# A planner's dearer transfers, and the first half batch of layer 0 entered on VectorE

## The chip, the cores and the metric

The kernel runs on one core of a Trainium2 chip, as one launch of one program. The metric is the device time of an execution in microseconds, lower being better; the time of a kernel is the median of several executions. A core has TensorE (matmuls, PE in the profile), VectorE (DVE), ScalarE (ACT), GpSimd (POOL) and SyncE (SP), which here does nothing but issue transfers. Each engine takes its instructions in the order in which they were written into the program and waits on semaphores where it needs another engine's result.

## The reference, cut to what matters

Four layers work on x of 2 batches of 1024 tokens of 128 features. Each normalises x, computes a sequence part s and a feed-forward part g, and adds their product:

```python
for layer in (L0, L1, L2, L3):
    xn = layernorm(x)
    x = x + layer.attn(xn) * silu(layer.ffn(xn))
```

Layer 0's sequence part is a selective recurrence, and its feed-forward part a mixture of eight experts of three products each:

```python
gated = clip(layernorm(x) @ sign(W1).T + b1, -1, 1)
x  = x + gated @ sign(W2).T + b2
qx = quantised(x)                        # by groups of tokens
u  = layernorm(qx)
xs, z = split(u @ in_proj.T)
xs = silu(causal_conv4(xs))
dt, B, C = split(xs @ x_proj.T)
dt = softplus(dt @ dt_proj.T + dt_b)     # 256 channels
h[t] = h[t-1] * exp(dt * A) + dt * xs * B   # 16 states a channel
y  = (h . C + D * xs) * silu(z)
out = qx + y @ out_proj.T
```

Layer 1 is an additive attention and eight gated experts, layer 2 a chunked state-space layer with 32 heads and eight small experts, layer 3 a causal attention and a two-product feed-forward. Only layer 0 has code that the change edits.

## The kernel before

**Layer 0.** The 2048 tokens are 16 tiles of 128, four quarters of 512, or two batches of two halves each. A half batch passes five stages, `take_1` to `take_5`. `take_1` takes the mean and variance of each of its four tiles of qx (`statistics`), the inverse root by three Newton steps (`inverse_root`), and writes `u` = qx * rinv + shift for each tile; then TensorE turns `u` (L632) and it is split into a rounded part `uT_h` and a rest `uT_l`. `take_2` does the convolution as 24 matmuls per half (two sets of 128 channels, four taps, three products each, tile `xz_ps`, helper `mm3` at L621 to L623) and the silu. `take_3` projects to dt, B and C and computes `e = exp(-|dt|)`. `take_4` computes the softplus as max(dt, 0) + ln(1 + e) with a correction `w = e - ((1 + e) - 1)` (L1080, L1081), the products `dt` and `dx` (L1084, L1085), and writes them to DRAM as `Dtd` (L1087), from where they are read back spread over partitions as `dd` (L1230). For the very first half and channel set, `dd` is read from SBUF instead (L1228), and no write stands before it. `take_5` does the gate z.

The recurrence is run in 16 steps a half batch (`inputs`, `step`): each has a product `dBx` = dx * B (L1243 on VectorE, one in four at L1241 on POOL), two exponentials `dA` on ACT (L1251), two scans of 128x512 on VectorE (L1252), two products with C on POOL (L1256) and four narrow matmuls that fold the states (L1263). B reaches the right partitions by a matmul `B_ps` (L1237). 128 scans in all make layer 0.

In `inverse_root`, the inverse root of a variance of four tiles runs Newton's steps on POOL (L595 to L598, four instructions a step); for other widths they run on VectorE (L591 to L593, three a step). `u` is written by POOL (L1007), and so are the two instructions of the softplus's correction.

Beside all this, layer 0's experts run on TensorE and ACT: `first` (L1137), `second` (L1142, L1144), `third` (L1152, L1154, L1156) and `weighted_sum` (L1162) for each of eight experts and four quarters, 32 tasks. Their weights are loaded by L1133. When the last task is done, `moe_end` (L1179 onward) makes the gate, which `layer_end` multiplies in.

**Layers 1 to 3.** Layer 1 of batch 0 begins while layer 0 still scans batch 1. Layer 2 works through 32 blocks (2 batches, 16 blocks of 128 channels), each with transfers of decays and rows (`so`, `cd`, `Srow`, `Mrow`) from DRAM scratch.

**What sets the order.** The program is first written in the order of the code. Then `_issue_order` takes all instructions and lists them anew for each engine. `_operations` gives each instruction a cost (`_price`), its dependences with lags, and, for a transfer, a time on the wire (`op.wire`, bytes by a rate that depends on the kind of source). `_forward` plays the engines with these costs: whenever an engine is free it takes, of its ready instructions, the one with the lowest key; a transfer takes its place on one common wire some time after its issue and is done some time after that, both parts of `_DMA`. `_backward` plays the program from its end, and its times are the next keys. Thirty rounds of this are made, then 300 tries with keys disturbed at random in a stretch of 60 us; the order with the shortest played span is kept and is written into the program as fixed order per engine. All transfers are issued by SyncE, one behind another; one that waits for its buffer or source holds those behind it.

So a changed price of transfers can change the order of every engine in every layer, and an instruction that moves to another engine changes the keys of those before it.

Of the kernel before, what the change touches and what calls it, by code (L numbers as in the profile page):

```python
# [15 lines left out]
ALU = mybir.AluOpType  # L16
# [56 lines left out]
_SAME = {"PE": -160.0, "DVE": 50.0, "Activation": 50.0, "Pool": 100.0, "SP": 0.0}  # L73
_TABLE = 1283.0
_SWITCH = 4000.0
_DMA = 1550.0
_SPELL = 3413.0
_LOW, _HIGH = 0.45, 0.8

# [73 lines left out]
def _operations(nc, slots):  # L153

    ops, users, past = [], {}, {}

    def in_psum(a):
        return a.tensor.name in slots and slots[a.tensor.name][3] == "PSUM"

    for ins in nc.cur_bb.bb.instructions:  # L160
        if type(ins).__name__.startswith("BassTile") or ins.opcode == "RegisterMove":
            continue
        op = _Op(len(ops), ins)
        reads, writes = ([a.bass_ap for a in x if getattr(a, "bass_ap", None) is not None] for x in (ins.ins, ins.outs))
        op.cost = _price(op, reads, writes, in_psum)
        op.table = _table_of(ins)
        op.columns, op.first, op.mate = set(), op, None
        if ins.opcode == "Matmult" and not ins.is_transpose and writes[0].ap[0][1] in (8, 32, 64):
            op.strip, op.area = writes[0].offset // (writes[0].ap[0][0] or 1), 1.0
            op.columns, op.strips = {(op.strip, writes[0].offset)}, {op.strip}  # L170
        op.wire = 0.0
        if op.dma:

            n, rows = 4, 1
            for _, c in writes[0].ap:
                n *= c
            again = any(s == 0 and c > 1 for s, c in reads[0].ap)
            for s, c in list(reads[0].ap)[:-1]:
                rows *= c if s else 1
            inside = reads[0].tensor.name in slots and slots[reads[0].tensor.name][3] != "DRAM"  # L180
            op.wire = n / (430.0 if not again else 200.0 if inside else 300.0 if rows > 2 else 170.0)
        for a, writing in [(a, False) for a in reads] + [(a, True) for a in writes]:
            name = a.tensor.name
            if name not in slots:
                continue
            space = slots[name][3]
            ap = [tuple(v) for v in a.ap]
            p0, p1, f0 = 0, 0, a.offset
            if space != "DRAM":
                row = _elements([(0, 0)] + [(0, d) for d in list(a.tensor.shape)[1:]])  # L190
                p0, f0 = divmod(a.offset, row)
                p1 = p0 + ap.pop(0)[1] - 1
            f1 = f0 + sum(abs(s) * (c - 1) for s, c in ap)
            if space == "PSUM":
                p0, p1, f0, f1 = 0, 127, 0, 4095
            log = past.setdefault(name, [])
            for q0, q1, g0, g1, other, wrote in log:
                if (writing or wrote or space == "PSUM") and other is not op and q0 <= p1 and p0 <= q1 and g0 <= f1 and f0 <= g1:
                    if other.engine != op.engine or other.dma:
                        lag = 0.0 if other.dma else _HOP[op.engine]  # L200
                    else:
                        lag = _SAME[op.engine] if wrote and not writing and op.engine != "PE" else -_AHEAD[op.engine]
                    op.after[other] = max(op.after.get(other, -1e3), lag)
            if writing:
                log[:] = [r for r in log if r[4] is op or not (p0 <= r[0] and r[1] <= p1 and f0 <= r[2] and r[3] <= f1)]
            log.append((p0, p1, f0, f1, op, writing))
            if name not in op.tiles:
                op.tiles.append(name)
                users.setdefault(name, []).append(op)
                if users[name][0] is not op:  # L210
                    op.after.setdefault(users[name][0], -1e3)

        mate = ops[-1] if ops else None
        if op.columns and mate is not None and mate.columns and mate.tiles[-1] == op.tiles[-1] and not mate.columns & op.columns:
            op.columns |= mate.columns
            if op.strip in mate.strips:
                op.cost += 10.0
            else:
                op.strips |= mate.strips
                op.cost = 25.0  # L220
            first = mate.first
            first.after.update({o: max(lag, first.after.get(o, -1e3)) for o, lag in op.after.items() if o.at < first.at})
            mate.mate, op.first = op, first
        ops.append(op)
    for op in ops:
        if op.columns and op.mate is None:
            op.cost += 87.0
    return ops, users
# [30 lines left out]
def _forward(ops, users, slots, behind, key):  # L259
# [22 lines left out]
    table, wire, port = None, 0.0, {"DVE": [0.0, 0.0], "Pool": [0.0, 0.0]}  # L282
# [24 lines left out]
    while events:  # L307
        now, kind, _, op = heapq.heappop(events)
# [17 lines left out]
        e = op.engine  # L326
# [6 lines left out]
        if held:  # L333
            op = mate
            ready[e].remove(held[0])
            heapq.heapify(ready[e])
        elif e == "PE" or e not in ("Activation", "DVE"):
            op = heapq.heappop(ready[e])[2]
        else:
            op = _next(ready[e], table, [max(0.0, t - now) for t in port["Pool"]] if e == "DVE" else (0.0, 0.0))  # L340
# [15 lines left out]
        idle[e] = now + (cost if e == "PE" or op.dma else max(cost - _AHEAD[e], 40.0))  # L356
        done = now + cost + (_AHEAD[e] if e == "PE" else 0.0)
        if op.dma:
            wire = max(wire, now + 0.4 * _DMA) + op.wire
            done = wire + 0.6 * _DMA  # L360
        end[op] = done
        for t in op.tiles:
            if t not in begun:
# [95 lines left out]
def recurrent_d4(ctx: ExitStack, tc: tile.TileContext, x, w0, f0, fwd, w1, w13d, w1y, w2, w2in, w3, r0, r2, r3, out):  # L459
    nc = tc.nc  # L460
# [105 lines left out]
    def tiles_of(b):  # L566
        return range(b * TPB, (b + 1) * TPB)

    def statistics(src, ts):

        n = len(ts)
        st = small.tile([P, n, 6], F32, name=f"ln_st{n}")
        mv = small.tile([P, n, 2], F32, name=f"ln_mv{n}")
        for i, t in enumerate(ts):
            nc.vector.bn_stats(st[:, i, :], src[:, t, :])
            nc.vector.bn_aggr(mv[:, i, :], st[:, i, :])
        return mv, inverse_root(mv[:, :, 1], f"ln{n}")

    def inverse_root(v, name):

        n = v.shape[-1]
        small_pool = n == 4
        x = small.tile([P, n], F32, name=f"{name}_x")
        nc.vector.tensor_scalar(x, v, EPS, None, ALU.add)
        y = small.tile([P, n], F32, name=f"{name}_y")
        yi = y.bitcast(I32)
        nc.vector.tensor_scalar(yi, x.bitcast(I32), 1, None, ALU.arith_shift_right)
        nc.vector.tensor_scalar(yi, yi, -1.0, 1597463007.0, ALU.mult, ALU.add)
        t = small.tile([P, n], F32, name=f"{name}_t")
        for _ in range(0 if small_pool else 3):  # L590
            nc.vector.tensor_tensor(t, y, y, ALU.mult)  # L591
            nc.vector.scalar_tensor_tensor(t, t, -0.5, x, ALU.mult, ALU.mult)
            nc.vector.scalar_tensor_tensor(y, t, 1.5, y, ALU.add, ALU.mult)  # L593
        for _ in range(3 if small_pool else 0):
            nc.gpsimd.tensor_tensor(t, y, y, ALU.mult)  # L595
            nc.gpsimd.tensor_tensor(t, t, x, ALU.mult)
            nc.gpsimd.tensor_scalar(t, t, -0.5, 1.5, ALU.mult, ALU.add)
            nc.gpsimd.tensor_tensor(y, t, y, ALU.mult)  # L598
        return y
# [225 lines left out]
    with ExitStack() as l1, ExitStack() as l0:  # L825
# [52 lines left out]
        with pool_of("l0a") as pa, pool_of("l0b", bufs=2) as pb, pool_of("l0_pre", bufs=5, space=PSUM) as pp:  # L878
# [118 lines left out]
            taken, held = {}, {}  # L997
            halo = pj.tile([P, 2, 3], F32R, name="halo")

            def take_1(b, h, pp, tag):  # L1000

                ts = range(b * TPB + 4 * h, b * TPB + 4 * h + 4)
                mv, rinv = statistics(qx, ts)
                shift = shifted(mv, rinv)
                u = pj.tile([P, 4, D], F32, name="u")
                for j, t in enumerate(ts):
                    nc.gpsimd.tensor_scalar(u[:, j, :], qx[:, t, :], rinv[:, j : j + 1], shift[:, j : j + 1], ALU.mult, ALU.add)  # L1007
                up = [pj.tile([P, 515], F32R, name=f"uT_{n}") for n in "hl"]
                for k, x in enumerate(up):
                    if h:  # L1010
                        nc.gpsimd.tensor_copy(x[:, 0:3], halo[:, k])
                    else:
                        nc.gpsimd.memset(x[:, 0:3].bitcast(F32), 0.0)
                split(turned(pp, u, tag), *(x[:, 3:] for x in up))
                if h == 0:
                    for k, x in enumerate(up):
                        nc.gpsimd.tensor_copy(halo[:, k], x[:, 512:515])
                held["up"] = up
# [52 lines left out]
            def take_4(b, h, pp, tag, fast=False):  # L1071
# [3 lines left out]
                for c in range(2):  # L1075
# [1 line left out]
                    ln = pp.tile([P, 512], F32, name="ln_ps", tag=tag)  # L1077
                    nc.scalar.activation(ln, e, AF.Ln, bias=one_col)

                    nc.gpsimd.tensor_scalar(w[:, c, :], e, 1.0, -1.0, ALU.add, ALU.add)  # L1080
                    nc.gpsimd.tensor_tensor(w[:, c, :], e, w[:, c, :], ALU.subtract)  # L1081
                    nc.vector.tensor_tensor(ln, ln, w[:, c, :], ALU.add)
                    nc.vector.scalar_tensor_tensor(ln, dt, 0.0, ln, ALU.max, ALU.add)
                    nc.scalar.copy(dt, ln)  # L1084
# [23 lines left out]
            routing(0, pp)  # L1108
            mark("first")
            quantise(0)  # L1110
            take_1(0, 0, pp, "mm")
            mark("routing_0")
            routing(1, pp)
            mark("first")
# [933 lines left out]
```

## Time and profile before

| what | value |
|---|---|
| median of three executions | 1190.09 us (1188.87 to 1194.23) |
| the profiled execution | 1188.86 us |
| its span | 1187.1 us |
| TensorE busy | 1020.7 us, 86% |
| VectorE busy | 931.5 us, 78% |
| ACT busy | 866.1 us, 73% |
| POOL busy | 739.2 us, 62% |
| mean granted TensorE clock | 0.939 |
| first scan starts | 126.73 us |
| last sum of layer 0's experts | 273.9 us |
| transfers | 109.09 MB, mean 92 GB/s |

The span is the time from the first to the last recorded instruction. A timeline line holds start, length, engine, code line, operation, what is written and read, count, and in brackets the idle time before it with what ended it. An SPq line is the issue of a transfer, not the transfer itself. A TensorE matmul in plain float32 stands as two records, one with float32r data as one. A busy TensorE under a granted clock below 1 is slower than its busy time says.

### The profile page before, as it was taken

To read this page: it belongs to the slowest core of one execution; us is meant where nothing else is said; L and a number is where in the kernel's file an instruction comes from. 1 tells how busy PE (TensorE), PEld (TensorE's weight loads), DVE (VectorE), ACT (ScalarE), POOL (GpSimd) and SP (SyncE) were. 2 spreads that over 40 slices of the span, in tenths; PEclk is the share of its full clock that TensorE was granted. 3 is DMA by queue.
4 is the path that set the end of the run, shared out by engine and by line. 5 is a ranking of instruction groups with operands and counts; after the bars stand their busy time and mean duration, and the time that the engine had idled before them with its cause. 6 is when DMAs were issued, how large, how long until landed. Compare 5 with 4: busy or idle time off the path is not lost.

```text
span 1187.1 us, 18167 instructions
## 1 busy us (share of the span) xinstructions
PE 1020.7 (86%) x6399; PEld 735.6 (62%) x6399; DVE 931.5 (78%) x1537; ACT 866.1 (73%) x1294; POOL 739.2 (62%) x776
## 2 busy tenths in 40 slices
PE   3997967979376889989779789999998999998998
PEld 2664523435033666778658576867676777776787
DVE  6734798997899896675776488888888999888666
ACT  4556785785877894574847689888898988877654
POOL 6564598895987375232151158797995978899311
PEclk9998997999567989999959899999999999999999
DMA  3003445352552113020030333445354444442000
GB/s 109 8 21 101 125 120 182 123 186 99 189 177 83 51 62 100 1 82 23 5 106 32 87 100 96 111 119 149 101 141 95 125 107 112 107 111 73 19 9 28
DMA packets 58846, 109.09 MB, mean 92 GB/s; under 512 B 6274, under 2 KB 31746, under 8 KB 58628
## 3 DMA queue, kind: packets, MB, share of 16 engines
q1 hardware_dynamic: 58756, 107.93, 31.6%
q8 instruction: 51, 0.84, 0.3%
q14 instruction: 39, 0.32, 0.1%
HBM read 91.52 MB, written 14.29 MB: 89 GB/s over the span
## 4 chain that ended last, share of the span: by engine, by line
PE 34%; DVE 10%; ACT 9%; issue 4%; DMA 3%; POOL 2%; SPq 0%; POOLq 0%; DVEq 0%; ACTq 0%
PE wo_ps L1781 4%; PE yd_ps L1757 3%; PE u_ps L1734 3%; PE yo_ps L1762 3%; DVE h L1419 2%; PE e_ps L1698 2%; PE y_ps L799 2%; DVE st L1735 2%; PE ht_ps L1719 1%; DMA so<-So 1%; PE y_ps L1895 1%; PE y_ps L1646 1%; PE av_ps L1925 1%; ACT e_ps L1699 1%; DVE M L1701 1%
## 5 line engine op out<-in xcount | busy, mean ns | idle before, releaser
L1256 POOL TENSOR_TENSOR hs<-hs,bc 128x512 f32<-128x512 f32 x128 | 161.0, 1278 | 48.6 <-DVE hs L1252 28.8
L1419 DVE SCALAR_TENSOR_TENSOR h<-in_ps,w,h 128x1023 f32<-128x1023 f32 (+2 forms) x96 | 121.1, 1271 | 5.7 <-ACT h L1416 5.5
L1251 ACT ACTIVATE dA<-dd,negA 128x512 f32<-128x512 f32 x128 | 87.4, 688 | 31.8 <-DVE hs L1252 25.4
L1735 DVE TENSOR_TENSOR_SCAN st<-cd,u_ps 128x512 f32<-128x512 f32 x64 | 77.8, 1215 | 19.4 <-PE u_ps L1734 8.7
L1701 DVE SCALAR_TENSOR_TENSOR M<-e_ps,GT 128x1024 f32<-128x1024 f32 x64 | 77.0, 1214 | 10.5 <-ACT e_ps L1699 10.3
L1768 POOL TENSOR_TENSOR h<-h,so 128x384 f32<-128x384 f32 (+1 forms) x64 | 73.0, 1144 | 19.1 <-DVE so L1767 18.6
L1769 POOL TENSOR_TENSOR h<-h,sg 128x512 f32<-128x512 f32 x64 | 82.9, 1300 | 0.8
L1252 DVE TENSOR_TENSOR_SCAN hs<-dA,last,dBx 128x512 f32<-128x512 f32 x64 | 79.9, 1271 | 2.9 <-ACT dA L1251 2.0
L799 PEld LDWEIGHTS y_ps<-w2e,hh 128*128 128x128 f32 x512 | 72.4, 199 | 14.7 <-DVE hh L791 3.8
L799 PE MATMUL y_ps<-w2e,hh 128*128 128x128 f32 x512 | 78.1, 288 | 1.9 <-DVE acc L804 0.9
L1723 POOL TENSOR_TENSOR hdd<-htok,dtd 128x512 f32<-128x512 f32 x64 | 67.1, 1051 | 20.3 <-ACT htok L1722 15.4
L1774 POOL TENSOR_TENSOR ssq<-ssq,so 128x512 f32<-128x512 f32 x60 | 76.6, 1286 | 3.0 <-ACT so L1773 2.9
L1757 PE MATMUL yd_ps<-M,htok 128*64 128x128 f32 x1024 | 70.7, 280 | 8.0 <-DVE M L1701 5.6
L1252 DVE TENSOR_TENSOR_SCAN hs<-dA,dBx 128x512 f32<-128x512 f32 x64 | 75.7, 1211 | 2.1 <-ACT dA L1251 1.1
L1734 PEld LDWEIGHTS u_ps<-hdd,Btok 128*128 128x128 f32 x448 | 63.3, 193 | 16.8 <-issue 6.0
L1762 PE MATMUL yo_ps<-Cf,stc 128*128 128x128 f32 x448 | 70.7, 280 | 2.1 <-DVE h L1765 0.9
L1734 PE MATMUL u_ps<-hdd,Btok 128*128 128x128 f32 x448 | 69.8, 281 | 2.8 <-POOL stc L1737 1.3
L1762 PEld LDWEIGHTS yo_ps<-Cf,stc 128*128 128x128 f32 x448 | 62.3, 191 | 13.4 <-issue 4.7
L1757 PEld LDWEIGHTS yd_ps<-M,htok 128*64 128x64 f32 x1024 | 55.1, 137 | 24.4 <-issue 7.0
L1243 DVE TENSOR_TENSOR dBx<-dd,B_ps 128x1024 f32<-128x1024 f32 x48 | 57.9, 1209 | 12.2 <-PE xz_ps L623 4.7
L1699 ACT ACTIVATE e_ps<-e_ps 128x1024 f32<-128x1024 f32 x64 | 64.3, 1011 | 1.9 <-PE e_ps L1698 1.4
L1263 PE MATMUL y_ps<-hs,fold 128*32 128x512 f32 x256 | 52.9, 758 | 14.1 <-DVE ln_t L591 9.2
(535 smaller groups left out, 3190.7 us busy)
## 6 DMA issues: line engine op xcount, KB each, us to landing
bc<-BCd SPq DMA_DIRECT2D x32, 512.0 KB
cd<-Dd SPq DMA_DIRECT2D x32, 512.0 KB
so<-So SPq DMA_DIRECT2D x64, 256.0 KB
dd<-Dtd SPq DMA_DIRECT2D x28, 512.0 KB
w13f<-in_w13d_dram SPq DMA_DIRECT2D x16, 256.0 KB
Dtd<-dt SPq DMA_DIRECT2D x7, 512.0 KB
fw<-in_fwd_dram SPq DMA_DIRECT2D x16, 192.0 KB
dd<-dt SPq DMA_DIRECT2D x4, 512.0 KB
```

Source lines behind the costliest of these rows:

```text
L799: nc.tensor.matmul(y_ps[:, j * P : (j + 1) * P], hh[:, c, j * P : (j + 1) * P], w2e[:, c * P : (c + 1) * P], start=(c == 0), stop=(c == 1))
L1251: nc.scalar.activation(dA, dd[:, r, 0, :], AF.Exp, scale=negA[:, n, r : r + 1])
L1252: nc.vector.tensor_tensor_scan(hs[:, r, :], dA, dBx[:, r, :], last[:, n, r : r + 1] if h else 0.0, ALU.mult, ALU.add)
L1256: nc.gpsimd.tensor_tensor(hs[:, r, :], hs[:, r, :], cs[:, 0, :], ALU.mult)
L1419: nc.vector.scalar_tensor_tensor(dst[:, n:], ps[:, : S - n], w[:, k : k + 1], dst[:, n:], ALU.mult, ALU.add)
L1701: nc.vector.scalar_tensor_tensor(M, ps, 3.0e38, G, ALU.min, ALU.mult)
L1734: nc.tensor.matmul(pv[:, j, :], Btok[:, c, :], hdd[:, c, :], start=True, stop=True)
L1735: nc.vector.tensor_tensor_scan(st.rearrange("p f j -> p (f j)"), cd[:, half].rearrange("p h w -> p (h w)"), ps, 0.0, ALU.mult, ALU.add)
L1757: nc.tensor.matmul(yd[64 * k : 64 * (k + 1), j * P : (j + 1) * P], htok[:, 4 * q + j, 64 * k : 64 * (k + 1)], Ms[q][:, k, j * P : (j + 1) ...
L1762: nc.tensor.matmul(yo[:, j * P : (j + 1) * P], stc[:, c - 1, :], Cf[:, c * P : (c + 1) * P], start=True, stop=True)
L1769: nc.gpsimd.tensor_tensor(y, y, sg[:, cols], ALU.mult)
L1774: nc.gpsimd.tensor_tensor(ssq[:, cols], ssq[:, cols], so[:, cols], ALU.add)
```

## The change

Two things are edited.

In the planner, the fixed price of a transfer goes from 1550 to 2150 ns; of this, 0.6 instead of 0.4 lie before the wire and 0.4 instead of 0.6 behind it. The rates of the wire fall from 430 to 300 bytes per ns for plain transfers, from 200 to 190 for one spread from SBUF, from 300 to 230 for one spread from many DRAM rows; 170 stays.

In the first half batch of batch 0 alone (`take_1(0, 0, ..., True)` and the `take_4` that was already called with True), Newton's steps, the four instructions that write `u`, and the four of the softplus's correction run on VectorE instead of POOL. All other half batches keep theirs on POOL.

```diff
-_DMA = 1550.0
+_DMA = 2150.0
...
-            op.wire = n / (430.0 if not again else 200.0 if inside else 300.0 if rows > 2 else 170.0)
+            op.wire = n / (300.0 if not again else 190.0 if inside else 230.0 if rows > 2 else 170.0)
...
-            wire = max(wire, now + 0.4 * _DMA) + op.wire
-            done = wire + 0.6 * _DMA
+            wire = max(wire, now + 0.6 * _DMA) + op.wire
+            done = wire + 0.4 * _DMA
...
-    def statistics(src, ts):
+    def statistics(src, ts, fast=False):
...
-        return mv, inverse_root(mv[:, :, 1], f"ln{n}")
-
-    def inverse_root(v, name):
+        return mv, inverse_root(mv[:, :, 1], f"ln{n}", n == 4 and not fast)
+
+    def inverse_root(v, name, aside=False):
...
-        small_pool = n == 4
...
-        for _ in range(0 if small_pool else 3):
+        for _ in range(0 if aside else 3):
...
-        for _ in range(3 if small_pool else 0):
+        for _ in range(3 if aside else 0):
...
-            def take_1(b, h, pp, tag):
+            def take_1(b, h, pp, tag, fast=False):
...
-                mv, rinv = statistics(qx, ts)
+                mv, rinv = statistics(qx, ts, fast)
...
-                    nc.gpsimd.tensor_scalar(u[:, j, :], qx[:, t, :], rinv[:, j : j + 1], shift[:, j : j + 1], ALU.mult, ALU.add)
+                    (nc.vector if fast else nc.gpsimd).tensor_scalar(u[:, j, :], qx[:, t, :], rinv[:, j : j + 1], shift[:, j : j + 1], ALU.mult, ALU.add)
...
-                    nc.gpsimd.tensor_scalar(w[:, c, :], e, 1.0, -1.0, ALU.add, ALU.add)
-                    nc.gpsimd.tensor_tensor(w[:, c, :], e, w[:, c, :], ALU.subtract)
+                    eng = nc.vector if fast else nc.gpsimd
+                    eng.tensor_scalar(w[:, c, :], e, 1.0, -1.0, ALU.add, ALU.add)
+                    eng.tensor_tensor(w[:, c, :], e, w[:, c, :], ALU.subtract)
...
-            take_1(0, 0, pp, "mm")
+            take_1(0, 0, pp, "mm", True)
```

## The prediction

> **What bounds the kernel now.** I read the page first (the span of 1187.1 us, the engines' shares, the chain that ended last), then the busy time of each engine by stage, then the timelines of POOL, VectorE, SyncE's queue and TensorE around the first scan, because the edits stand there. The profiled execution took 1188.86 us, 1.76 us more than its span and 1.23 us less than the median of 1190.09 us.
>
> The busy time by stage (length, then busy us and count of each engine, TensorE's granted clock, DMA share, GB/s):
>
> ```profile
> core 0: us, PE busy (x) PEld busy (x) DVE busy (x) ACT busy (x) POOL busy (x), PEclk, DMA share, GB/s
> ...
> 20.00:82.00 62.00, 57.95 (x348) 39.40 (x348) 38.12 (x101) 36.43 (x67) 42.01 (x81) 1.00 0.05 14
> 82.00:127.00 45.00, 35.33 (x157) 23.22 (x157) 16.25 (x30) 24.39 (x40) 12.60 (x25) 0.89 0.42 109
> 127.00:276.00 149.00, 124.45 (x682) 62.62 (x681) 134.49 (x136) 111.51 (x193) 131.53 (x113) 0.94 0.43 142
> 276.00:400.00 124.00, 83.02 (x335) 41.45 (x334) 111.31 (x163) 95.84 (x160) 91.57 (x70) 0.72 0.39 130
> 400.00:680.00 280.00, 241.90 (x1436) 194.62 (x1435) 192.84 (x459) 183.28 (x279) 92.47 (x103) 0.92 0.19 55
> 680.00:1040.00 360.00, 342.95 (x2498) 263.08 (x2497) 319.20 (x363) 314.46 (x407) 284.79 (x277) 1.00 0.44 113
> ```
>
> The reader is to see three kinds of stage. From 680 to 1040 us (layer 2) TensorE is 95% busy at full clock and bounds. From 127 to 400 us (layer 0's scans) VectorE is 90% busy and TensorE waits at a lower clock. From 20 to 127 us the recurrence has not begun: TensorE is full until 82 us with the expert work of layer 0, then nothing is full; VectorE is 36% busy between 82 and 127. The chain of waits reaches back only to 433 us and says nothing on the start.
>
> What holds the first scan up, on POOL, then VectorE, then SyncE's queue, then TensorE:
>
> ```profile
> 55.06 0.63 POOL L595 TENSOR_TENSOR ln_t<-ln_y 128x4 f32<-128x4 f32 x1
> ...
> 70.61 0.20 POOL L598 TENSOR_TENSOR ln_y<-ln_t,ln_y 128x4 f32<-128x4 f32 x1
> ...
> 72.65 1.75 POOL L1007 TENSOR_SCALAR u<-qx,ln_y,shift 128x128 f32<-128x128 f32 x4
> ...
> 99.75 3.84 POOL L1080 TENSOR_SCALAR sp_w<-sp_e 128x512 f32<-128x512 f32 x2
> 103.55 2.49 POOL L1081 TENSOR_TENSOR sp_w<-sp_e,sp_w 128x512 f32<-128x512 f32 x2
> ```
>
> ```profile
> 50.84 1.89 DVE L1103 TENSOR_SCALAR qx<-qx,rg 128x256 f32<-128x256 f32 x1
> ...
> 104.85 0.70 DVE L1082 TENSOR_TENSOR ln_ps<-ln_ps,sp_w 128x512 f32<-128x512 f32 x1 [4.26 <-POOL sp_w L1081]
> ...
> 109.31 1.28 DVE L1085 TENSOR_TENSOR dt<-ln_ps,xs 128x512 f32<-128x512 f32 x2
> ...
> 125.47 1.22 DVE L1243 TENSOR_TENSOR dBx<-dd,B_ps 128x1024 f32<-128x1024 f32 x1 [4.70 <-PE xz_ps L623]
> 126.73 2.34 DVE L1252 TENSOR_TENSOR_SCAN hs<-dA,dBx 128x512 f32<-128x512 f32 x2
> ```
>
> ```profile
> 110.02 0.33 SPq L1087 DMA_DIRECT2D Dtd<-dt  x1
> 110.62 1.25 SPq L1228 DMA_DIRECT2D dd<-dt  x2
> 112.68 3.30 SPq L1230 DMA_DIRECT2D dd<-Dtd  x1
> 116.02 3.18 SPq L1228 DMA_DIRECT2D dd<-dt  x2
> ```
>
> ```profile
> 70.51 1.12 PE L1142 MATMUL p<-h,fw 128*128 128x512 f32 x2
> ...
> 82.14 0.50 PE L621 MATMUL xz_ps<-uT_h,taps_l 128*128 128x512 f32 x1
> ```
>
> Newton's steps lie on POOL from 55.06 to 70.81 us, twelve instructions of 0.2 us scattered among large ones; `u` follows, and the convolution starts at 82.14. The softplus's sum waits 4.26 us for POOL. dBx at 125.47 is charged to TensorE, but its B_ps matmul was done by 115.9. It also needs both halves of `dd`; the halves of one tile are not issued together (the first pair at 110.62 is the first half of two tiles, the second pair at 116.02 their second halves), so I read this wait as the transfer.
>
> **Part 1, Newton's steps and u on VectorE.** Removed from POOL: 12 instructions and four `u` (1.75 us). Added to VectorE: nine of about 0.17 us (row L593 at 18.3 to 20.4 us), 1.5, and four 128x128 tensor-scalars at 0.25 to 0.34 (row L917), 1.1. In the new order they stand among routing's instructions; counting these with their rows on from the copy of probs at 57.05, the last `u` ends near 61.4 us, not 74.36. But TensorE was full, so what counts is what it does ahead of the convolution. In the built order there are 61 fewer matmuls ahead: nine of L621 to L623 at 0.235 (2.1), three of L1142 at 1.05 (3.2; the row's two records are one matmul), four of L1152 at 0.43 (1.7), thirteen of L1154 at 0.23 (3.0), 32 of L1162 at 0.083 (2.6): 12.6 us. 82.14 becomes 69.5, and u's transposes come up near 63, after 61.4. The two accounts agree, so -12.6 us. Queued behind `u` on VectorE is routing's second maximum; it gets 1.1 us later, beside full TensorE work.
>
> **Part 2, the softplus's sums.** POOL's four instructions took 6.3 us, begun after `u` of the other half. On VectorE two tensor-scalars at 0.41 to 0.48 (rows L1105, L896) and two tensor-tensors at 0.69: 2.3 us, from the end of the exponential at 98.20 to 100.5. Then the logarithm is late: a table load of 1.28 us and a first half that ends at 100.8. So 104.85 becomes 100.8, -4.05. The new order also puts two zs products and a uT_l (107.52 to 109.31, 1.8 us) behind the first L1085. Together -5.9 us for the issue of `dd`. Nothing that stands behind the new instructions on VectorE is needed earlier.
>
> **Part 3, the order of transfers.** In SyncE's queue the first two `dd` now stand ahead of the Dtd write, and the first tile's second half stands before the `dd` that has to wait until Dtd has landed (3.30 us at 112.68). An expert's weight load stands ahead of them and waits for TensorE's eighth third-layer product, which comes some 4 us before by its place in the order. Bounds: 0 (the transfers share the same engines) and -5.4 (116.02 less 110.62). I take -2: the number of 512 KB transfers ahead falls by one, not by all. First scan: 126.73 - 12.6 - 5.9 - 2 = 106.2 us, 20.5 earlier.
>
> **What goes back.** TensorE work ahead of the first B_ps falls by 11.1 us (nine, four, three, twelve and eight of the kinds above); it has to lie beside the scans. There TensorE has 149 - 124.45 = 24.6 us free, part of its busy time is at clock 0.94, and VectorE and POOL have 15 and 17 free. Bounds 0 and +11.1; I take +4, as three engines near 90% can't be interleaved without loss.
>
> **The rest of the plan.** The price moves every instruction's key, so all is ordered anew. The expert sum's end stands behind 66 scans instead of 68, the last scan behind 18 products of layer 1's experts in both, and TensorE's work ahead of the first and of the 256th L1757 is the same within 2 us. The activation tables are loaded 155 times, not 163: 8 x 1.283 us of ACT, which bounds nowhere before 400 us. Bounds for all of this: -10.3 (all loads on the path) and, from the queue in layer 2, +22 (below). I take 0.
>
> Sum: -20.5 + 4 + 0 = -16.5. 1188.86 - 16.5 = 1172.4 for a profiled execution, 1173.6 at the median; I say 1174 us, 1.4% faster.
>
> **A rule against it.** The tensor-scalar L1103 at 50.84 took 1.89 us and ended 0.14 us after POOL's taps_l product (50.22 to 52.59); without POOL beside it the 128x512 form took 0.41. The Trainium skill (SBUF — State Buffer, Who interferes with whom) says that such instructions and GpSimd's take a shared port pair in turn, the loser blocked for the whole instruction; the trace agrees. By that rule each of the six moved tensor-scalars could stand behind a POOL instruction of 1.27 us: 7.6 us, and the sum would be -8.9, 1181 at the median. I keep the rows' uncontended times, since POOL has little left to run there.
>
> **Rivals.** *The gain is eaten beside the scans.* All 11.1 us come back, and port waits or `dd` landing no sooner cost 2 to 5 more: -20.5 + 11.1 + 3 = -6.4, so 1184 (1182 to 1188). For it: 90% on VectorE, 88% on POOL. Against: TensorE's 24.6 us. That the change does not move the scan at all (TensorE stays in the way) speaks against the 61 matmuls; 5.9 us of part 2 would remain, also 1184. *Slower: SyncE's queue in layer 2.* A dearer transfer is issued earlier; at the head of an in-order queue it waits for its buffer, and the loads behind it wait too. SyncE's L1692 waited 97.8 us in 25 waits for its buffer already. Layer 2 has 32 block steps with TensorE 95% busy: each us lost per block costs up to 32. It cancels the gain at 0.5 us a block and is slower by 0.5% from 0.7 (22 us): 1196 to 1205. Against it: TensorE's order there is unchanged.
>
> **The numbers.** Forecast 0.62; eaten, or scan not moved, 0.17; queue 0.17; 0.04 for more gain than forecast, when the chain's 3% of DMA (36 us) shrinks too. The forecast's own range: 1174 with Part 3's -3.4 and no loss (-4) below, 1166, and the whole +11.1 above (+7.1) and +2 of Part 3, 1183. The range reaches down to 1160 and up through the eaten case to the edge of the queue's, 1197. Half a per cent (6 us) is about what this measurement can tell, as the three runs spread by 0.45%. Faster: 0.62 + 0.04 + 0.03 of the eaten case, 0.69; same 0.14; slower 0.17.
>
> **What would show it.** Right: convolution near 70 us, no wait for POOL at L1082, first scan at 104 to 109, expert end near 256 to 262, TensorE's share of the span up by about a point. Wrong: a first scan after 115, a scan stage longer than 153 us, or TensorE under 94% from the first L1757 to the last.

## The result, and the profile after

The changed kernel takes 1203.51 us at the median of four executions (1199.79 to 1208.90), the kernel before 1190.78 us (1188.87 to 1194.23). The ratio is 1.0125, with a 95% interval of 1.0082 to 1.0168: slower by 1.25%. I had forecast 1174 us and a range that ended at 1197. The profiled execution took 1199.79 us, the least of the four; its span is 1198.1 us.

The busy time by stage of the changed kernel (length, then busy us and count of each engine, TensorE's granted clock, DMA share, GB/s). The limits are the first convolution, the first scan, the experts' last sum, 400 us as in the table before, and the first and last L1757:

```profile
core 0: us, PE busy (x) PEld busy (x) DVE busy (x) ACT busy (x) POOL busy (x), PEclk, DMA share, GB/s
20.00:68.00 48.00, 44.62 (x239) 32.57 (x239) 33.08 (x90) 29.88 (x55) 30.11 (x42) 1.00 0.03 9
68.00:109.00 41.00, 34.93 (x195) 23.31 (x195) 20.92 (x56) 23.84 (x39) 13.82 (x43) 0.92 0.46 112
109.00:252.00 143.00, 128.01 (x725) 67.14 (x725) 127.39 (x127) 116.17 (x201) 126.31 (x111) 0.96 0.45 150
252.00:400.00 148.00, 93.34 (x337) 43.97 (x335) 131.53 (x172) 93.93 (x158) 103.03 (x79) 0.69 0.34 116
400.00:683.00 283.00, 239.86 (x1446) 194.95 (x1445) 191.44 (x458) 170.82 (x273) 86.07 (x98) 0.93 0.17 52
683.00:1104.00 421.00, 399.04 (x2887) 303.56 (x2886) 372.49 (x417) 362.01 (x468) 334.81 (x327) 0.99 0.41 109
```

The first two stages are shorter, as forecast (48 and 41 us instead of 62 and 45); the third is shorter too (143 instead of 149), where I had forecast it longer by 4. The fourth starts 24 us earlier and is where the lead is lost: up to 400 us it has 337 matmul records in 148 us at a clock of 0.69, where the kernel before had 335 in 124 us at 0.72. The last one is longer: from the first L1757 to the last 421.5 us instead of 414.4.

The start of the recurrence did what the change says. TensorE's first convolution product, then VectorE's timeline, then SyncE's queue of the changed kernel (start, length, engine, line, operation, tiles, count, idle time before and what ended it; the lines quoted from 583 to 1078 are one less than before):

```profile
68.06 0.50 PE L620 MATMUL xz_ps<-uT_h,taps_l 128*128 128x512 f32 x1
```

```profile
59.31 2.25 DVE L1006 TENSOR_SCALAR u<-qx,ln_y,shift 128x128 f32<-128x128 f32 x4
...
86.81 0.76 DVE L1080 TENSOR_SCALAR sp_w<-sp_e 128x512 f32<-128x512 f32 x2 [1.08 <-ACT sp_e L1067]
...
89.30 1.31 DVE L1082 TENSOR_TENSOR ln_ps<-ln_ps,sp_w 128x512 f32<-128x512 f32 x2 [0.25 <-ACT ln_ps L1077]
...
92.34 0.69 DVE L1085 TENSOR_TENSOR dt<-ln_ps,xs 128x512 f32<-128x512 f32 x1 [0.54 <-ACT dt L1084]
...
107.99 1.22 DVE L1243 TENSOR_TENSOR dBx<-dd,B_ps 128x1024 f32<-128x1024 f32 x1 [3.58 <-DMA dd<-dt]
109.24 2.34 DVE L1252 TENSOR_TENSOR_SCAN hs<-dA,dBx 128x512 f32<-128x512 f32 x2
```

```profile
93.06 1.23 SPq L1228 DMA_DIRECT2D dd<-dt  x2
94.39 4.31 SPq L1087 DMA_DIRECT2D Dtd<-dt  x1
98.75 4.23 SPq L1228 DMA_DIRECT2D dd<-dt  x2
```

The first scan starts at 109.24 instead of 126.73, 17.5 us earlier, and the experts' last sum (L1162) is at 251.5 instead of 273.9. But the first sum of layer 0 into X (L1288), from which layer 1 of batch 0 begins, moves only from 306.85 to 299.96. The gate `g` (L1285) is loaded into the buffer that `bc_rows` of the last half batch holds until it is written out; so it goes by the recurrence's pace, not the experts'.

In SyncE's queue `bc_rows` is written out 12 us earlier (282.75 instead of 294.85) and `g` loaded 10 us earlier (287.64 instead of 297.56). The traces of three runs below with the same order up to there (e9, e11, e12) put this first sum between 298 and 307 us, so the 7 us are themselves uncertain by about as much.

Two sights in the fourth and fifth stage stand out. The first is a VectorE instruction on 128x8 numbers that takes 7 us. VectorE's timeline, then POOL's:

```profile
313.21 6.96 DVE L583 TENSOR_SCALAR ln_x<-ln_mv 128x8 f32<-128x8 f32 x1
320.08 1.21 DVE L1243 TENSOR_TENSOR dBx<-dd,B_ps 128x1024 f32<-128x1024 f32 x1
```

```profile
310.83 6.17 POOL L1256 TENSOR_TENSOR hs<-hs,bc 128x512 f32<-128x512 f32 x5
316.96 0.74 POOL L609 TENSOR_TENSOR qk_w_l<-w,qk_w_h 128x264 fp32r<-128x264 f32 x1
317.66 2.48 POOL L609 TENSOR_TENSOR w_l<-w13f,w_h 128x512 fp32r<-128x512 f32 x2
324.60 2.49 POOL L1256 TENSOR_TENSOR hs<-hs,bc 128x512 f32<-128x512 f32 x2 [4.46 <-ACT last L1254]
```

L583 is the first step of layer 1's inverse root and took 1.82 us before (at 319.80). It ends at 320.17, when POOL's unbroken row of eight instructions ends (320.14), not when one of them does. In these 7 us VectorE scans nothing.

The second is a pause of 33 us in the scans, between the 120th and the 121st of the 128. VectorE, then TensorE, then ScalarE:

```profile
404.95 1.28 DVE L1252 TENSOR_TENSOR_SCAN hs<-dA,last,dBx 128x512 f32<-128x512 f32 x1
...
436.12 0.74 DVE L1269 SCALAR_TENSOR_TENSOR y<-xs,w,y_ps 128x512 f32<-128x512 f32 x1
...
438.12 1.28 DVE L1252 TENSOR_TENSOR_SCAN hs<-dA,last,dBx 128x512 f32<-128x512 f32 x1 [0.67 <-PE y_ps L1263]
```

```profile
433.53 1.06 PE L1277 MATMUL o_ps<-w,y 128*128 128x128 f32 x8
...
434.87 1.06 PE L1277 MATMUL o_ps<-w,y 128*128 128x128 f32 x8
...
437.02 1.06 PE L1263 MATMUL y_ps<-hs,fold 128*32 128x512 f32 x8
```

```profile
371.82 0.60 ACT L789 ACTIVATE hh<-pg 128x512 f32<-128x512 f32 x1
...
397.34 0.69 ACT L1251 ACTIVATE dA<-dd,negA 128x512 f32<-128x512 f32 x1 [8.61 <-DVE hs L1252]
...
399.54 0.60 ACT L789 ACTIVATE hh<-pg 128x512 f32<-128x512 f32 x1
...
420.43 0.69 ACT L1251 ACTIVATE dA<-dd,negA 128x512 f32<-128x512 f32 x1
```

The bracket of the scan at 438.12 names what released it: the folding matmuls (L1263), not an exponential. The exponentials of this scan and the next were done by 416.3 and 421.1; the later ones need a buffer that these two scans give back. Read backwards with the code's buffers, the chain is: the scan writes into an `hs` that the folding has to read first; the folding starts a new `y_ps`, 0.16 us after L1269 has read the old one; L1269 writes into the only `y`, 0.19 us after the third half batch's output projection (L1277) has read it. That projection's input had been ready since 354.18. In TensorE's order it stands behind products of layer 1's experts, so here the recurrence goes by layer 1's pace. In the kernel before it ended at 431.24 and the 121st scan began at 433.67, but there the 120th came as late as 429.83 and no pause shows.

Layer 1's experts pause too. Their sixth and seventh activation `hh` stand 27.7 us apart in ScalarE's timeline (20.3 in the kernel before), though the seventh's input was done at 374.12: it stands behind layer 1's attention and behind exponentials of the recurrence that wait for scans, 8.61 us the last time. So two layers wait for one another in queues of fixed order. The recurrence, still 19 us ahead after 112 scans (the next starts at 379.2 instead of 398.5), starts its last scan 4.5 us later than before (452.3 instead of 447.8), and the last sum of layer 0 is at 467.5 instead of 464.5. Behind it the program takes 730.6 us instead of 722.5.

### The profile page after: what moved, and what is told of

Its sections match the earlier page's. It is cut to its first block, busy times and chain, and to the rows that moved or that the text cites. A ratio compares the mean times of both kernels' runs of the same rounds, so it can differ in the third digit from the quotient of the medians.

```text
span 1198.1 us, 18162 instructions
## 1 busy us (share of the span) xinstructions
PE 1028.0 (86%) x6399; PEld 739.7 (62%) x6399; DVE 950.3 (79%) x1554; ACT 854.1 (71%) x1286; POOL 728.5 (61%) x756
## 4 chain that ended last, share of the span: by engine, by line
PE 34%; ACT 16%; DVE 16%; issue 5%; POOL 2%; DMA 1%; SPq 0%; POOLq 0%; DVEq 0%; ACTq 0%
PE y_ps L798 3%; PE u_ps L1734 3%; PE wo_ps L1781 3%; PE yd_ps L1757 3%; PE yo_ps L1762 2%; DVE h L1419 2%; DVE hs L1252 2%; DVE st L1735 2%; ACT L789 2%; ACT e_ps L1699 2%; PE ht_ps L1719 1%; PE e_ps L1698 1%; ACT L1699 1%; PE y_ps L1646 1%; PE y_ps L1895 1%
## 5 line engine op out<-in xcount | busy, mean ns | idle before, releaser
L1723 POOL TENSOR_TENSOR hdd<-htok,dtd 128x512 f32<-128x512 f32 x64 | 67.0, 1049 | 24.9 <-ACT htok L1722 24.3
L798 PE MATMUL y_ps<-w2e,hh 128*128 128x128 f32 x512 | 75.5, 284 | 3.9 <-DVE hh L790 1.5
L798 PEld LDWEIGHTS y_ps<-w2e,hh 128*128 128x128 f32 x512 | 69.5, 196 | 13.4 <-DVE hh L790 4.5
L1757 PE MATMUL yd_ps<-M,htok 128*64 128x128 f32 x1024 | 70.9, 281 | 2.6 <-DVE M L1701 2.2
L789 ACT ACTIVATE hh<-pg 128x512 f32<-128x512 f32 x64 | 37.5, 597 | 48.9 <-PE pg L622 48.6
L1263 PE MATMUL y_ps<-hs,fold 128*32 128x512 f32 x256 | 54.6, 708 | 18.4 <-POOL hs L1256 18.3
L1757 PEld LDWEIGHTS yd_ps<-M,htok 128*64 128x64 f32 x1024 | 55.3, 138 | 17.3 <-issue 5.1
```

The costliest lines, as they stand in the source:

```text
L798: nc.tensor.matmul(y_ps[:, j * P : (j + 1) * P], hh[:, c, j * P : (j + 1) * P], w2e[:, c * P : (c + 1) * P], start=(c == 0), stop=(c == 1))
L1757: nc.tensor.matmul(yd[64 * k : 64 * (k + 1), j * P : (j + 1) * P], htok[:, 4 * q + j, 64 * k : 64 * (k + 1)], Ms[q][:, k, j * P : (j + 1) ...
```

## The experiments

Theory A was that the dearer price costs and the entry gains; rival B that the entry itself costs; rival C that the planner's rounds end in another order after any small change, and that the order found for 2150 ns is a poor one whatever its edits are for. Ratios are to the kernel before, with 95% intervals; 1% is 11.9 us.

### One edit at a time, and another seed of the search

```diff
 # e1: only the entry on VectorE; e2: only the planner's prices
 # e3 (changed kernel) and e4 (kernel before):
-    rng = random.Random(1)
+    rng = random.Random(2)
```

> The VectorE entry alone (Newton's steps, u and the softplus's sums of the first half batch), with the old prices of transfers. Theory A, the new price makes the loss and the entry gains: first scan near 107 to 110 us as with both edits, and 1170 to 1180 us (before, 1190, less 10 to 20). Rival B, the entry itself costs, because its work moved beside the scans and because TensorE then idles earlier at a lower clock: first scan near 109 as well, but 1195 to 1205. Rival C, the loss is a chance of the order that the search happened to find, so either edit can land anywhere within about 10 us of 1190.

> The new prices of transfers alone, the entry on POOL as before. Theory A: the first scan stays at 120 to 127 us, and the time is 1200 to 1215 us, that is the loss of 13 us of both edits plus the entry's gain that is not there. Rival B: 1185 to 1193. Rival C: within about 10 us of 1190 on either side, and the next two runs move as much.

> The changed kernel, with another seed of the order's random search and nothing else; same instructions, another order. Theory A and rival B both give 1198 to 1209 us, as the cause would be in the price or the entry. Rival C gives a time that differs from 1203.5 by 6 us or more.

> The kernel before, with another seed of the order's random search and nothing else. Theory A and rival B: 1185 to 1195 us. Rival C: a time that differs from 1190 by 6 us or more, in which case a single comparison of two orders says little of the edits.

The entry alone gave 1.0106 (1.0061 to 1.0152), the price alone 1.0142 (1.0090 to 1.0195). The other seed gave 1.0158 (1.0115 to 1.0201) for the changed kernel and 0.9989 (0.9967 to 1.0011) for the one before. So each edit costs by itself, and together they cost no more than either: effects that do not add. The first scans came at 112.6 with the entry alone (107 to 110 expected) and at 124.7 with the price alone (120 to 127 expected). Theory A's gain for the entry fell. Rival B was right on the entry alone and wrong on the price alone (1185 to 1193 us expected, 1203.9 measured). Rival C fell in the form in which I had put it, as the seed changes little (0.1 and 0.3%); that is what one would see if the 300 tries only disturb what the thirty rounds have found. (The profiled execution of the entry alone, 1185.87 us, was the fastest of its five; its trace alone would have misled.)

### A price 50 ns away

```diff
 # e5, kernel before
-_DMA = 1550.0
+_DMA = 1600.0
 # e6, changed kernel
-_DMA = 2150.0
+_DMA = 2100.0
 # e7: e1 with random.Random(2)
 # e8, changed kernel with the old rates
-            op.wire = n / (300.0 if not again else 190.0 if inside else 230.0 if rows > 2 else 170.0)
+            op.wire = n / (430.0 if not again else 200.0 if inside else 300.0 if rows > 2 else 170.0)
```

> The kernel before with the fixed price at 1600 instead of 1550 ns and nothing else, 3% of its value. Theory A, a dearer transfer itself makes the order worse: the loss of 13 us for 600 ns and new rates would give 1 us here, so 0.998 to 1.004 of the kernel before. Rival C, the planner's thirty rounds end in another order after any change of a price, and the kernel before holds one of the better ones: a ratio outside 0.995 to 1.005, more likely above.

> The changed kernel with a fixed price of 2100 instead of 2150 ns and nothing else. Theory A: 1.010 to 1.017 of the kernel before, as the changed kernel. Rival C: anything from 0.995 to 1.025, by more than 0.5% another value than the changed kernel's 1.0125.

> The VectorE entry alone with the old prices, and another seed of the random search; it repeats the run of the entry alone, whose five times ran from 1186 to 1201 us. If the entry itself costs: 1.006 to 1.015 of the kernel before, with the first scan near 112 us, 14 us early, and the last sum of layer 0 later or no more than 8 us earlier than before. If the entry alone gains as the trace of that run (1184 us) reads: 0.990 to 1.000.

> The changed kernel with the old rates of the wire (430, 200, 300 bytes per ns) but the new fixed price of 2150 ns and its new split. Theory A with the fixed price as the cause: 1.010 to 1.017 of the kernel before. Theory A with the rates as the cause: 0.99 to 1.005. Rival C: any of these, and the loss does not sit in the same stage as in the changed kernel.

e5 gave 1.0014 (0.9981 to 1.0047), no difference, against rival C for this one price. e6 gave 0.9829 (0.9771 to 0.9888), 1166.98 us: the changed kernel with a price 2% lower is 3% faster than the changed kernel, and faster than my forecast. e8 gave 0.9885 (0.9842 to 0.9928). e7 gave 1.0048 (1.0017 to 1.0080), between its two predictions; the entry alone costs less than e1 said, but does not gain. Its first scan came at 122.0, not near 112: another seed's order alone took back most of the entry's lead. Theory A cannot give e6. The two programs hold the same instructions; only their order differs.

In e6 POOL has a row too, from 307.42 to 313.61, but there VectorE got in between its first two products (VectorE, then POOL, of e6):

```profile
307.96 0.77 DVE L583 TENSOR_SCALAR ln_x<-ln_mv 128x8 f32<-128x8 f32 x1
```

```profile
307.42 3.73 POOL L1256 TENSOR_TENSOR hs<-hs,bc 128x512 f32<-128x512 f32 x3
```

### Where the two orders differ by 36 us

The orders of the changed kernel and of e6 were written into the program as lists, so that they could be joined. "Front" is everything up to the last sum of layer 0.

```diff
-    for n in range(rounds + tries):
-        ...
-        start, end, orders, taken = _forward(ops, users, slots, behind, key)
+    for at in struct.unpack(f"<{len(raw) // 2}H", raw):
+        orders.setdefault(ops[at].engine, []).append(ops[at])
 # e9: the list is the changed kernel's front, then e6's order
 # e10: e6's front, then the changed kernel's order
 # e11: the changed kernel's order up to layer 1's L583, then e6's
 # e12: the changed kernel's order; the 13 small VectorE instructions from L583 on in one row, and
+        if n == 8 and not seen_once:
+            seen_once.append(nc.gpsimd.tensor_copy(small.tile([P, n], F32, name="seen"), y))
```

> The changed kernel's program, its order given as a list instead of planned: up to the last sum of layer 0 (X at 467.5 us) the order of the changed kernel, from there on the order that the price of 2100 ns gave. If the loss sits where the two traces differ: 22 us of the 34 in the front part and 12 behind it, so the front's loss stays and the rest goes: a span of 1183 to 1189, median 0.995 to 1.005 of the kernel before. If layer 2's order were the whole cause: about 0.983.

> The reverse: up to the last sum of layer 0 the order that the price of 2100 ns gave, from there on the changed kernel's. Last sum of layer 0 at 444 to 447 us, the rest 12 us longer than with 2100: a span of 1174 to 1179, median 0.990 to 0.998 of the kernel before. If a late front is what makes the later order slow, it would instead be 0.983 to 0.986.

> The changed kernel's order only up to the first instruction of layer 1's inverse root (L583, at 313 us in the changed kernel, where it took 6.96 us), then the order that 2100 gave. If the loss begins at 313 us: last sum of layer 0 at 445 to 452 and a span of 1164 to 1171, median 0.983 to 0.990 of the kernel before. If it is already in what stands before 313 us (the expert sums or the late gate): last sum after 460 and a span over 1180.

> The changed kernel's order with one stretch mended: the thirteen small VectorE instructions of layer 1's first inverse root stand together, and one tiny GpSimd copy that reads their result is put into GpSimd's order ahead of its long row of products, so that GpSimd stops for them. If L583's 6.96 us are time in which GpSimd's unbroken row keeps VectorE out: L583 takes under 1.4 us, the row of thirteen ends near 316 us instead of 337, and the kernel is 5 to 11 us faster than the changed one, 1.003 to 1.008 of the kernel before. If the wait is of no weight because TensorE and ScalarE keep their order: L583 is short, but the time stays within 3 us of the changed kernel. If L583 stays at 7 us, the row of GpSimd is not what holds it.

e9 gave 1.0027 (0.9997 to 1.0058) and e10 0.9918 (0.9883 to 0.9952), both as expected. Of the 2.96% between the changed kernel and e6, the order behind layer 0 is worth 0.9 to 1.0% (e10 less e6; changed kernel less e9), 11 us, and the front 2.0%, 24 us; the two add up. (By the intervals, each of these differences is uncertain by 0.4 to 0.7%.) The traces agree: behind the last sum of layer 0 e6's order took 718.3 us in e6 and 721.4 in e9, the changed kernel's 730.6 there and 729.2 in e10.

e11 gave 0.9920 (0.9889 to 0.9952), above the 0.983 to 0.990 that I had expected for a loss that begins at 313 us; its profiled execution, the slowest of ten, has the last sum at 464.3, as I had expected for a loss that is there before. Set against e6, 0.9% or 11 us of the front's loss is already in the order up to there, which still holds POOL's row (L583 took 7.06 us in e11 too); some 13 us are in the order between 313 us and the last sum.

The surest sight of these 13 us is e9 beside e11. They ran together, their orders differ only between L583 and the last sum of layer 0, and their medians are 13.1 us apart (1194.37 and 1181.25). In their traces what follows the last sum is alike (721.4 and 722.5 us). The sixth and seventh `hh` of layer 1 are 27.7 us apart in e9 and 10.9 in e11 (10.9 in e6), the projection L1277 ends at 441.99 and 431.33 (412.69 in e6), and the last sum comes at 475.1 and 464.3. In the traces of all twenty orders the 121st scan starts 2.2 to 4.7 us after that projection ends, and the last sum 24.7 to 31.5 us after that scan. So this stretch of the order costs the 13 us; that it does so by the place of `hh` in ScalarE's queue is read from the traces, and was not tried by moving it alone.

e12 gave 1.0054 (1.0025 to 1.0082), 0.7% or 8 us below the changed kernel's ratio; the two intervals just touch. VectorE's timeline and POOL's of e12 (its lines are up to three higher):

```profile
311.21 0.16 DVE L584 TENSOR_SCALAR ln_x<-ln_mv 128x8 f32<-128x8 f32 x1
...
313.63 0.17 DVE L606 SCALAR_TENSOR_TENSOR shift<-ln_mv,ln_y 128x8 f32<-128x8 f32 x1
```

```profile
308.82 2.50 POOL L1259 TENSOR_TENSOR hs<-hs,bc 128x512 f32<-128x512 f32 x2
313.66 0.19 POOL L600 COPY seen<-ln_y 128x8 f32<-128x8 f32 x1 [2.34 <-PE xz_ps L625]
313.81 3.73 POOL L1259 TENSOR_TENSOR hs<-hs,bc 128x512 f32<-128x512 f32 x3
```

The instruction takes 0.16 us, the row of thirteen 2.6 us instead of the 24 us from L583 to `shift` in the changed kernel, and the last sum of layer 0 comes at 462.5 instead of 467.5. So L583 is short where POOL is made to stop; the row of thirteen was drawn together at the same time, so the 8 us belong to both edits. They were not the main loss: the scans' pause stayed, from 399.3 to 433.1, with `hh` 28.5 us apart.

### What the entry and the price are worth

```diff
 # e13: the mending of e12 in e6's order
 # e14: kernel before, split 0.6/0.4, new rates
+_DMA = 2100.0
 # e15: kernel before, split 0.6/0.4, old rates
+_DMA = 2150.0
 # e16: e6's order as a list, the entry back on GpSimd
-            take_1(0, 0, pp, "mm", True)
+            take_1(0, 0, pp, "mm")
 #      and the softplus's sums of take_4 likewise
 # e17, e18: changed kernel with
+_DMA = 2050.0
+_DMA = 2200.0
```

> The order that the price of 2100 gave, with the same mending as before: layer 1's first inverse root in one row on VectorE and a tiny GpSimd copy ahead of GpSimd's products. There L583 and the next one took 0.77 and 0.64 us, not 6.96. If the mending gains by the blocked time alone: 0 to 2 us, 0.981 to 0.984 of the kernel before. If it gains by the shorter row (16 us from the first of the thirteen to xn): 4 to 9 us, 0.975 to 0.980.

> The kernel before with a price of 2100 and the new rates and split, the entry on GpSimd. With the entry this price gave 0.983. If the price makes the gain there and the entry nothing: 0.980 to 0.988. If the entry makes it: 0.993 to 1.003. Rival C, every price has its own order with and without the entry: 0.98 to 1.02, no use of either rule.

> The kernel before with a price of 2150, the new split and the old rates, the entry on GpSimd. With the entry these prices gave 0.9885. If the entry is worth 1 to 1.5% in a typical order: 0.997 to 1.005. If the entry is worth nothing: 0.985 to 0.992.

> The order that the price of 2100 gave with the entry, as a list, but with Newton's steps, u and the softplus's sums back on GpSimd (at the same places of the order by its times), TensorE's, ScalarE's and SyncE's order unchanged. First scan some 10 to 20 us later than 113.8. If the entry's gain reaches the end: 10 to 18 us slower than with the entry, 0.991 to 0.998 of the kernel before. If the scans' lead is lost in the stretch up to layer 1's start, where the lead of 17.5 us had shrunk to 7: 3 to 8 us, 0.985 to 0.990. If it is of no worth: 0.982 to 0.985.

> The changed kernel with a fixed price of 2050 ns. 2100 gave 0.983 of the kernel before and 2150 1.0125. If the time has a trend in the price: 0.978 to 0.988, near 2100's. If each price gives an order of its own (rival C): anywhere from 0.98 to 1.015, with GpSimd's row ahead of L583 or not, and no VectorE instruction of over 4 us where the time is below 0.99.

> The changed kernel with a fixed price of 2200 ns. Trend: 1.010 to 1.025, at or above 2150's 1.0125. Rival C: anywhere from 0.98 to 1.015, and at least one of this run and 2050's away from its neighbour by more than 1%.

| price of a transfer | without the entry | with the entry |
|---|---|---|
| 1550, old rates and split | 1 (other seed 0.9989) | 1.0106 (other seed 1.0048) |
| 1600, old rates and split | 1.0014 | not run |
| 2050, new rates and split | not run | 0.9962 (0.9934 to 0.9991) |
| 2100, new rates and split | 1.0100 (1.0059 to 1.0142) | 0.9829 (0.9771 to 0.9888) |
| 2150, old rates, new split | 1.0063 (1.0032 to 1.0093) | 0.9885 (0.9842 to 0.9928) |
| 2150, new rates and split | 1.0142 (1.0090 to 1.0195) | 1.0125 (1.0082 to 1.0168) |
| 2200, new rates and split | not run | 0.9892 (0.9827 to 0.9958) |

The last two runs settle the trend: from 2050 to 2200 ns the time goes 0.996, 0.983, 1.0125, 0.989. That is no slope. 2150 with the new rates stands out from both neighbours by more than 2%, so its slowness belongs to the order found there, which is rival C. e14 (1.0100) lies in rival C's range alone, and e15 (1.0063) above both of its ranges. Without the entry the three dearer prices are all slower, by 0.6 to 1.4%; with it four of five are faster than the kernel before, by 0.4 to 1.7%. The difference that the entry makes at one price runs from +1.1% to -2.7%. (The pause of the scans, too, comes and goes with the order: 29.7 us or more from scan to scan in seven traces, at ratios from 0.996 to 1.016; the seven orders below 0.993 have 11.7 to 17.7 us there. But the entry alone and the price alone are slow without it.) A part of my expectation for e17 and e18 failed: e17 and e18 have the long L583 too, and e18 is fast all the same:

```profile
303.92 6.95 DVE L583 TENSOR_SCALAR ln_x<-ln_mv 128x8 f32<-128x8 f32 x1
```

e16 gives the entry's own worth with the order held: 0.9867 (0.9830 to 0.9903), beside 0.9829 for e6 and 0.9821 (0.9785 to 0.9857) for e13, which ran with e16. That is 5 us by the ratios, with intervals that overlap, and 9 us by the two traces. The ratio falls where I expected it if part of the lead were lost before layer 1 starts, but the traces show no such loss. First scan on VectorE and last sum on POOL, of e6 and of e16:

```profile
113.81 2.34 DVE L1252 TENSOR_TENSOR_SCAN hs<-dA,dBx 128x512 f32<-128x512 f32 x2
```

```profile
445.44 1.29 POOL L1288 TENSOR_TENSOR X<-X,g 128x512 f32<-128x512 f32 x1
```

```profile
121.99 2.34 DVE L1252 TENSOR_TENSOR_SCAN hs<-dA,dBx 128x512 f32<-128x512 f32 x2
```

```profile
453.76 1.29 POOL L1288 TENSOR_TENSOR X<-X,g 128x512 f32<-128x512 f32 x1
```

8.2 us at the first scan are 8.3 us at the end of layer 0 and 9.0 at the end of the program (spans of 1163.7 and 1172.8). By these traces a lead at the first scan arrives whole where the order does not lose it; by the ratios about half of it does. e13 shows that mending a row that does not block gains nothing: it is the same as e6. e6 and e13 are the fastest of all, and both beat both kernels.

## Why the prediction was wrong, step by step

**Part 1** (-12.6 us) was right (-14.1 measured): the convolution starts at 68.06 (forecast 69.5), and the last `u` ends at 61.56 (forecast 61.4), the latter with some luck, as two of the new instructions took longer than forecast (below). **Part 2** (-5.9) measured -2.9: from the first convolution product to the first L1085 24.3 us instead of 27.2. The 4 us for the softplus's sum were right (from the end of the exponential to L1082 2.5 us instead of 6.7, and no wait for POOL), but the way from the convolution to the exponential's end became 2.7 us longer. **Part 3** (-2, bounds 0 and -5.4) measured its bound of 0: from the first `dd` to the first scan 16.2 us as against 16.1, the second pair still waiting behind the Dtd write (4.31 us at 94.39). Sum to the first scan -17.5 instead of -20.5, which is just past the edge of the 104 to 109 that I gave.

**What goes back** (+4) did not by the end of the experts: from the first scan to the last L1162 142.2 us instead of 147.2, TensorE at 0.96 instead of 0.94. Their end at 251.5 was ahead of my 256 to 262.

**The rest of the plan** (taken as 0, bounds -10.3 and +22) is the step that failed. -16.5 forecast and +12.7 measured are 29 us apart, more than even the bound of +22 allowed. By the traces the front of the program, which should have gained 16.5, lost 3.0 (last sum of layer 0 at 467.5 instead of 464.5), and the part behind it lost 8.0 (730.6 instead of 722.5). I had compared the built orders at a few places: scans ahead of the experts' end, products of layer 1 ahead of the last scan, TensorE's work ahead of the first and 256th L1757. None of these sees which instructions stand ahead of one another in three queues between 313 and 440 us. What the runs showed in place of the 0: the scans' lead ended there, as the 121st scan waits, through L1269, for a projection that stands behind layer 1's experts, and these stood still for 27.7 us. Against e6's order this stretch cost 13 us, and L583's row some 8 more by e12 (the two were not tried together); about 11 us arose behind layer 0. The count of table loads that I had taken for a possible gain (155 instead of 163) means little: e6 has 155 too.

**The rule that I weighed.** I had kept the uncontended times because POOL had little left to run at the entry. For the softplus's sums that held: their two tensor-scalars took 0.76 us. For the start it did not. The third of the four `u` took 1.63 us beside a POOL instruction of 1.71 (the others 0.34), and one Newton step 1.26 instead of 0.17 (VectorE, then POOL):

```profile
57.81 1.26 DVE L592 SCALAR_TENSOR_TENSOR ln_y<-ln_t,ln_y 128x4 f32<-128x4 f32 x1
```

```profile
57.79 1.26 POOL L658 TENSOR_TENSOR room<-room,before 128x512 f32<-128x512 f32 x1 [1.50 <-DVE ln_t L591]
```

Together they lost 2.4 us; by the rule I had worked out up to 7.6. The Trainium skill (SBUF — State Buffer, Who interferes with whom) says that whoever is first holds the shared ports for the whole of its instruction and the other is blocked that long. Both waits agree with it: they ended 0.08 and 0.02 us after that POOL instruction. L583, 250 us later, differs in its length: it was kept out for six further instructions of POOL after the one that ran when it came up, 6.96 us where the rule's single instruction would be 1.27.

**The rivals.** The gain eaten beside the first scans was not it. The slower rival had the right number (1196 to 1205) by the wrong mechanism: SyncE's L1692 waited 69.2 us for its buffer from 683 to 1104 us, 91.0 in the faster e6. The blocks of layer 2 lost 0.2 us each, not 0.7. None of my three signs of a wrong prediction came up: the first scan was before 115, the scan stage shorter than 153 us, TensorE at 94.8% from the first L1757 to the last. They all lay where I had worked out a price, and none in the stretch that I had taken as 0.

**What stays open.** In layer 2 e6's order has TensorE busy for 391.5 of 411 us and the changed kernel's for 399.0 of 421, with the same matmuls; the 7.5 us are spread over many of them, and no wait of one kind answers to them. Between 313 and 440 us the two pauses are where the time is seen, but neither `hh` nor the projection was moved by itself. What makes the entry alone and the price alone slow was not followed up.

## What to carry to other kernels

A planner that searches can make the constant in its price a dice throw: here, around 2150 ns, 50 ns or 2% moved the time by 3% one way and 2.3% the other (from 1550 to 1600 by nothing that could be told), while the seed of its final search moved it by 0.1 to 0.6%. An edit to such a kernel is judged by several neighbouring settings or with the order held as a list, and a forecast for one of them needs a range for the order alone, however well the edit's own terms are worked out; I estimate 1.5% to either side, from the 0.983 to 1.0125 of the five dearer prices with the entry. A lead at the start of a long chain is worth its full size only as far as the in-order queues behind it keep it; look for the first instruction that stands behind another stage's work.

## What the runs showed of the hardware

A small VectorE instruction was kept out beside GpSimd for longer than one GpSimd instruction. L583 on 128x8 took 6.96 us beside an unbroken row on POOL and ended 0.03 us after its last instruction. In seven of the twenty traces it took 6.85 to 8.02 us, and ended 0.03 or 0.04 us after POOL's row each time; in the others it took 0.16 (POOL made to wait, e12) to 1.82 us. In e6 it got in at the first boundary, after 0.77 us, with POOL's instructions as close together. What decides between these two was not found.
